# A LayerNorm chain over three chunks instead of two, with its input read a second time by halves

## The chip, the cores and the metric

The kernel runs on one core of a Trainium2 chip. The metric is device microseconds (us) of one execution. A core has five engines that run side by side: PE (TensorE, matmuls), DVE (VectorE), ACT (ScalarE), POOL (GpSimd) and SP (SyncE, which here only issues transfers). Each takes its own instructions in order. Transfers (DMA) run on 16 DMA engines; they are issued from SP's queue, a few from ACT's and POOL's. SBUF and PSUM are the on-chip memories, the second the one that matmuls write to; DRAM is outside.

## The reference, cut to what matters

Four images of 96 x 128 x 128 go through two layers. Layer 0 normalizes by groups, projects to 192 channels, convolves, and runs four directional scans (state space model). Their sum `ym` is normalized over its 192 channels pixel by pixel (LayerNorm), projected back to 96 channels and added to x. Layer 1 then works on that sum with convolutions and an attention whose products act as convolution weights. The change lies in the end of layer 0:

```python
yn = jnp.moveaxis(ym, 1, -1)
mu = yn.mean(-1, keepdims=True)
var = yn.var(-1, keepdims=True)
yn = (yn - mu) * jax.lax.rsqrt(var + 1e-05) * ln_w + ln_b
yn = jnp.moveaxis(yn, -1, 1)
return jnp.einsum('bdhw,cd->bchw', yn, out_w) + out_b[None, :, None, None]
...
x = x + _L0_conv_ref(_gn(x), ...)
x = x + _L1_conv_ref(_gn(x), ...)
```

## The kernel before, in words

The program is a sequence of generators whose steps are interleaved. `co_run(left, right, pace)` (L291) takes a step of `left`, whose `yield` gives a cost, and then steps of `right` until cost times pace is used up. Where LayerNorm stands in it:

- image 0: `ssm_output` and then `split_norm` are `left`, the scan of the second image pair (`ssm_scan`, steps of 2.6) is `right`, with a pace of 0.65 (L2501 and L2502). Up to the end of the scan the order of emission is kept on each engine (`in_order`, L328 and L2507).
- image 1: it is `right` beside `direct_maps` of image 0 (3 x 3 convolutions as matmuls, L2119), with a pace of 1.0 (L2512 to L2516).
- images 2 and 3: it is `right` beside the attention of the image before (matmuls of L1488 and L1503, evacuations from L1542 on), with a pace of 1.0 (L2544 to L2564), and followed by `split_norm` of the same image and `attn_output` of an earlier one.

From image 1 on, the tile framework orders the instructions of each engine itself, by emission and by its own estimate of when each is ready.

`ssm_output` (L924) takes an image in NS = 16 chunks of SN = 1024 pixels. The 192 channels lie as two halves (j = 0, 1) on 96 partitions. The mean is folded into the weights (`outws`), so that the projection can be made of the raw y and scaled afterwards. A chunk c goes through these steps:

- `load_y` (L936): y, 96 x 2 x 1024 float32, 768 KB, issued on SP; three buffers.
- `squares` (L941): the squares of each half, on ACT.
- `sums` (L946): matmuls of y and of the squares with a 32-column block of 1/192, in one bank of PSUM: mean and mean square of each pixel.
- `rows` (L960): ACT copies the bank to SBUF and issues two transfers that turn it into `mq`, 8 rows of 128 pixels for mean and mean square.
- `inverse` (L967) on DVE and `roots` (L973) on ACT: variance and its root; `back` (L977): the reciprocal on DVE, its transfer to DRAM (`rd`, issued on POOL), and the load of the input image `xr` on SP; `spread_out` (L993): `rd` read back to all 96 partitions as `r`, issued on POOL. L1072 adds the output's constant to `xr` on ACT.
- `projected` (L999): for each half h of 512 pixels two matmuls of y with `outws`; `scaled` (L1011): times r, on DVE; `added` (L1019): plus xr, on POOL; `counted` (L1027): statistics for the next layer, on DVE; then the store to `xnew` (L1078) on SP.

For images 1 to 3 (`turned`) the sum stands in `r`, for image 0 in `xr`. PSUM banks come from a pool of three for image 0 and of two for the others (L2509); the bank of the sums and those of the two projections take turns. In the loop (L1034) round c has the chunks new = c, mid = c - 1 and old = c - 2, and six pauses. Other tiles of `ssm_output` have two buffers, `st` one.

`split_norm` (L1081) then reads `xnew` twice; its second pass (L1247 among others) writes the planes that the attention reads.

Of the kernel before, what the change touches and what calls it, by code (L numbers as in the profile page):

```python
# [9 lines left out]
F32 = mybir.dt.float32  # L10
BF16 = mybir.dt.bfloat16
AF = mybir.ActivationFunctionType
# [5 lines left out]
C = 96  # L18
H = W = 128
L = H * W  # L20
CH = 512
NCH = L // CH
# [29 lines left out]
SN = 1024  # L52
NS = L // SN
# [16 lines left out]
def kernel(  # L70
# [26 lines left out]
    nc = tc.nc  # L97
# [180 lines left out]
    def bank(ps):  # L278

        return ps.tile([128, CH], F32, name="bank", tag="bank")  # L280

    def part(ps, *shape):
        n = 1
        for d in shape[1:]:
            n *= d
        t = bank(ps)[: shape[0], :n]
        return t if len(shape) == 2 else t.rearrange("p (a b) -> p a b", b=shape[2])
# [636 lines left out]
    def ssm_output(b, yms, xnew, stats, ps, side, turned):  # L924

        with tc.tile_pool(name="c2", bufs=2, side=side) as p2:  # L930
            xb = x[b].rearrange("c h w -> c (h w)")
            ym = yms.rearrange("(j p) l -> p j l", j=2)
            rd = dram.tile([L], F32, name="rd")
            ys, sums_of, near, made = {}, {}, {}, {}

            def load_y(c):  # L936
                if c < NS:
                    ys[c] = p2.tile([C, 2, SN], F32, name="y", bufs=3)
                    nc.sync.dma_start(ys[c], ym[:, :, bass.ts(c, SN)])

            def squares(c, j):  # L941
                sq = p2.tile([C, SN], F32, name="sq")
                nc.scalar.activation(sq, ys[c][:, j], AF.Square)
                sums_of[c, j] = sq

            def sums(c, j):  # L946
                sq = sums_of.pop((c, j))
                if j == 0:
                    sums_of[c] = bank(ps)
                pm = sums_of[c]  # L950
                for g in range(4):
                    rhs = sq if g % 2 else ys[c][:, j]
                    nc.tensor.matmul(
                        pm[32 * g : 32 * g + 32],
                        lhsT=mean192[:, 0:32],
                        rhs=rhs[:, bass.ts(g // 2, CH)],
                        start=(j == 0),
                        stop=(j == 1),
                    )
            def rows(c):  # L960
                st = p2.tile([128, CH], F32, name="st", bufs=1)
                nc.scalar.copy(st, sums_of.pop(c))
                mq = made[c] = p2.tile([RS, 2, W], F32, name="mq")
                for i in range(2):
                    nc.scalar.dma_start(mq[:, i], st[32 * i : 32 * i + 65 : 64])

            def inverse(c):  # L967
                m, q = made[c][:, 0], made[c][:, 1]
                nc.vector.tensor_mul(m, m, m)
                nc.vector.tensor_sub(q, q, m)  # L970
                nc.vector.tensor_scalar(q, q, 0.0, None, ALU.max)

            def roots(c):  # L973
                q = made[c][:, 1]
                nc.scalar.activation(q, q, AF.Sqrt, bias=eps[0:RS])

            def back(c):  # L977
                m, q = (made[c][:, i] for i in range(2))
                made.pop(c)
                if turned:  # L980
                    nc.vector.reciprocal(
                        m.rearrange("p (j t) -> p t j", j=TW), q.rearrange("p (t j) -> p t j", j=TW)
                    )
                    q = m
                else:
                    nc.vector.reciprocal(q, q)
                to = rd[bass.ts(c, SN)]
                nc.gpsimd.dma_start(to.rearrange("(p f) -> p f", f=W), q)
                xr = p2.tile([C, SN], F32, name="xr")
                nc.sync.dma_start(xr, xb[:, bass.ts(c, SN)])  # L990
                near[c] = xr, to

            def spread_out(c):  # L993
                xr, to = near[c]
                r = p2.tile([C, SN], F32, name="r")
                nc.gpsimd.dma_start(r, to.partition_broadcast(C))
                near[c] = xr, r

            def projected(c, h):  # L999
                po = part(ps, C, CH)  # L1000
                for j in range(2):
                    nc.tensor.matmul(  # L1002
                        po,
                        lhsT=outws[:, j],
                        rhs=ys[c][:, j, bass.ts(h, CH)],
                        start=(j == 0),
                        stop=(j == 1),
                    )
                return po

            def scaled(c, h, po):  # L1011
                r = near[c][1][:, bass.ts(h, CH)]
                if turned:
                    v = r.rearrange("p (h j t) -> p h j t", t=TN, j=TW)
                    nc.vector.tensor_mul(v, turned_view(po), v)
                else:
                    nc.vector.tensor_mul(r, po, r)  # L1017

            def added(c, h):  # L1019
                xr, r = (t[:, bass.ts(h, CH)] for t in near[c])  # L1020
                if turned:
                    v = r.rearrange("p (h j t) -> p h j t", t=TN, j=TW)
                    nc.gpsimd.tensor_add(v, v, turned_view(xr))
                else:
                    nc.gpsimd.tensor_add(xr, r, xr)

            def counted(c, h):  # L1027
                t = near[c][turned]
                nc.vector.bn_stats(stats[:, 2 * c + h], t[:, bass.ts(h, CH)])

            for c in range(3):
                load_y(c)
            yield 2.0
            for c in range(NS + 2):  # L1034
                new, old = c < NS, c - 2 if c >= 2 else None
                mid = c - 1 if 1 <= c <= NS else None
                if old is not None:
                    po = projected(old, 0)
                if mid is not None:
                    inverse(mid)  # L1040
                if new:
                    squares(c, 0)
                yield 1.2
                if mid is not None:
                    roots(mid)
                if old is not None:
                    scaled(old, 0, po)
                    po = projected(old, 1)
                    ys.pop(old)
                if new:  # L1050
                    squares(c, 1)
                yield 1.4
                if mid is not None:
                    back(mid)
                if old is not None:
                    added(old, 0)
                    scaled(old, 1, po)
                if new:
                    sums(c, 0)
                yield 1.4  # L1060
                if new:
                    sums(c, 1)
                if old is not None:
                    added(old, 1)
                    counted(old, 0)
                    load_y(c + 1)
                yield 1.4
                if new:
                    rows(c)
                if mid is not None:  # L1070
                    xr = near[mid][0]
                    nc.scalar.activation(xr, xr, AF.Identity, bias=outbs)  # L1072
                    spread_out(mid)
                if old is not None:
                    counted(old, 1)
                yield 1.4
                if old is not None:
                    nc.sync.dma_start(xnew[:, bass.ts(old, SN)], near.pop(old)[turned])  # L1078
                yield 1.4

    def split_norm(xnew, x1d, x2d, stats, keep, cnt, ps, side, planes, vector, done):  # L1081
# [174 lines left out]
    def turned_view(v):  # L1256

        return v.rearrange("p (h t j) -> p h j t", t=TN, j=TW)
# [1134 lines left out]
    class Image:  # L2393
# [26 lines left out]
        def norm(self, yms, ps, side):  # L2420
            yield from ssm_output(self.b, yms, self.xnew, self.stats, ps, side, self.b > 0)
# [47 lines left out]
    with tc.tile_pool(name="wp", bufs=1, side="left") as wp:  # L2469
# [7 lines left out]
        for images, pace in (([0], 0.25), ([1], 0.75), ([2, 3], 1.35)):  # L2477
            left = projections(images, weights, stats, wp, psl)
            if images[0] == 0:
                next(left)  # L2480
                next(others)
                made = pair_weights()
# [12 lines left out]
                wdt, wbc, outws, outbs = got  # L2495
# [148 lines left out]
```

## Time and profile before

| what | value |
|---|---|
| runs | 6549.08, 6573.5, 6575.6 us (median 6573.5) |
| profiled execution | 6572.02 us, span 6570.2 us |
| mean granted TensorE clock | 0.884 |
| busy PE, DVE, ACT, POOL | 5365.0, 4934.7, 3806.4, 3533.2 us (82, 75, 58, 54%) |
| DMA over the span | 1198.29 MB, mean 182 GB/s |
| squares L943 | 128, from 2110.5 to 5076.0 us |
| sums L953 | 2 x 512 matmul instructions |
| projection L1002 | 512 matmul instructions, 717 ns each in the mean |
| loads of y, L939 | 64 of 768 KB, 374 ns of SP each (median) |

A busy share is an average over stages with different limits, and a row that gives idle time names what the engine waited for before an instruction. A wait on one engine costs time only if the engine that bounds the stage is held by it. Windows are given in us from the span's start.

### The profile page before, as it was taken

To read this page: it belongs to the slowest core of one execution; us is meant where nothing else is said; L and a number is where in the kernel's file an instruction comes from. 1 tells how busy PE (TensorE), PEld (TensorE's weight loads), DVE (VectorE), ACT (ScalarE), POOL (GpSimd) and SP (SyncE) were. 2 spreads that over 40 slices of the span, in tenths; PEclk is the share of its full clock that TensorE was granted. 3 is DMA by queue.
4 is the path that set the end of the run, shared out by engine and by line. 5 is a ranking of instruction groups with operands and counts; after the bars stand their busy time and mean duration, and the time that the engine had idled before them with its cause. 6 is when DMAs were issued, how large, how long until landed. Compare 5 with 4: busy or idle time off the path is not lost. (4 is left out here: it accounts for less than half of the span.)

```text
span 6570.2 us, 76328 instructions
## 1 busy us (share of the span) xinstructions
PE 5365.0 (82%) x23264; PEld 2348.1 (36%) x23264; DVE 4934.7 (75%) x7469; ACT 3806.4 (58%) x4757; POOL 3533.2 (54%) x2744
## 2 busy tenths in 40 slices
PE   6889988987887835999987588876979777888888
PEld 2333323322222112444433244444424454344553
DVE  3247778988898768989745884687865788887867
ACT  1247768777787676677524464565544664444542
POOL 2236758978788546979522454466134574043430
PEclk9999989998998657999998799877988887998899
DMA  6767777776766757665676776655776555865658
GB/s 162 175 155 189 193 208 195 217 204 163 217 184 172 215 157 228 202 201 173 201 188 167 194 198 176 168 140 145 211 194 165 144 158 153 225 164 146 182 149 217
DMA packets 888486, 1198.29 MB, mean 182 GB/s; under 512 B 216142, under 2 KB 741014, under 8 KB 875596
## 3 DMA queue, kind: packets, MB, share of 16 engines
q1 hardware_dynamic: 864460, 1138.46, 63.7%
q0 software_dynamic: 16208, 38.42, 2.2%
q10 hardware_dynamic: 7408, 16.53, 0.8%
q8 instruction: 187, 3.06, 0.2%
q14 instruction: 223, 1.83, 0.1%
HBM read 777.62 MB, written 345.58 MB: 171 GB/s over the span
## 5 line engine op out<-in xcount | busy, mean ns | idle before, releaser
L622 PE MATMUL bank<-y,wp 128*128 128x512 f32 (+3 forms) x3584 | 1317.3, 626 | 86.3 <-DMA y<-y 33.8
L855 POOL TENSOR_TENSOR y<-y,dl 128x1024 f32<-128x1024 f32 x384 | 1058.0, 2755 | 271.8 <-DVE dl L847 252.6
L822 POOL TENSOR_TENSOR dl<-dl,u 128x1024 f32<-128x1024 f32 x384 | 1011.7, 2635 | 248.8 <-ACT dA L798 124.2
L843 DVE TENSOR_TENSOR_SCAN dA<-dA,pBC 128x512 f32<-128x512 f32 x768 | 981.4, 1278 | 30.7
L1488 PE MATMUL two<-ya,wd 128*64 128x192 f32 (+3 forms) x2376 | 600.6, 433 | 216.1 <-ACT odd L1559 106.8
L622 PEld LDWEIGHTS bank<-y,wp 128*128 128x128 f32 (+3 forms) x3584 | 459.0, 169 | 757.6 <-issue 656.0
L2119 PE MATMUL bank<-y,wn 128*128 128x384 f32 (+5 forms) x2408 | 678.0, 508 | 60.6 <-DMA y<-x1d 28.1
L847 DVE TENSOR_TENSOR dl<-dA,pBC 128x512 f32<-128x512 f32 x768 | 528.1, 688 | 257.6 <-PE pBC L736 185.0
L736 PE MATMUL pBC<-xr,wbc 60*128 60x512 bf16 (+1 forms) x1536 | 463.0, 405 | 316.4 <-DVE dA L843 245.3
L1922 ACT COPY yb<-ya 64x768 f32<-64x768 f32 (+1 forms) x660 | 537.9, 815 | 185.5 <-PE two L1488 122.1
L665 ACT ACTIVATE dl<-pd,dtb 128x512 f32<-128x512 f32 x768 | 486.2, 684 | 190.6 <-PE pd L736 175.2
L1488 PE MATMUL two<-yb,wd 128*64 128x192 f32 (+3 forms) x2376 | 573.3, 416 | 0.0
L826 DVE TENSOR_TENSOR pBC<-dl,pBC 128x512 f32<-128x512 f32 x768 | 527.6, 687 | 8.3 <-POOL dl L822 7.4
L2119 PEld LDWEIGHTS bank<-y,wn 128*128 128x128 f32 (+3 forms) x2408 | 310.7, 169 | 357.7 <-issue 194.1
L1488 PEld LDWEIGHTS two<-ya,wd 128*64 128x64 f32 (+1 forms) x2376 | 269.9, 174 | 433.3 <-ACT odd L1559 116.4
L798 ACT ACTIVATE dA<-dl,negA 128x1024 f32<-128x1024 f32 x384 | 420.3, 1141 | 2.3
L2226 POOL MEMSET o<- 1x1024 f32 x60 | 56.5, 949 | 602.8 <-PE bank L2281 296.0
L1992 POOL COPY own<-ring 32x512 f32<-32x512 f32 (+1 forms) x198 | 227.3, 1184 | 278.8 <-DVE ring L1581 237.1
L736 PEld LDWEIGHTS <-wbc 60*128 60x128 bf16 (+1 forms) x1536 | 103.2, 96 | 765.0 <-issue 752.0
L665 ACT ACT_TABLE_LOAD x248 | 318.2, 1283 | 97.4 <-PE pd L736 83.6
L1488 PEld LDWEIGHTS two<-yb,wd 128*64 128x64 f32 (+1 forms) x2376 | 298.2, 176 | 149.0 <-issue 41.1
L1002 PE MATMUL bank<-y,outws 96*96 96x512 f32 x512 | 298.3, 717 | 5.5 <-DVE r L1017 2.7
(323 smaller groups left out, 9888.6 us busy)
## 6 DMA issues: line engine op xcount, KB each, us to landing
u<-zb SPq DMA_DIRECT2D x192, 1024.0 KB
yms<-y SPq DMA_DIRECT2D x96, 512.0 KB
y<-yms SPq DMA_DIRECT2D x64, 768.0 KB
xn<-xnew SPq DMA_DIRECT2D x128, 384.0 KB
ya<-vp SPq DMA_DIRECT2D x120, 336.0 KB
y<-y SPq DMA_DIRECT2D x128, 258.2 KB
zb<-z SPq DMA_DIRECT2D x64, 512.0 KB
ya<-x1p SPq DMA_DIRECT2D x90, 336.0 KB
```

The costliest lines, as they stand in the source:

```text
L622: nc.tensor.matmul(blocks(pz[p:e]), lhsT=ws[k][:, d, c : c + e - p], rhs=window(ys[k], at, d, n), start=(i == 0), stop=(i == len(terms) - 1),)
L665: nc.scalar.activation(dst, src, AF.Softplus, bias=bias)
L736: nc.tensor.matmul(p, lhsT=w[rows], rhs=xr[rows, at : at + CH], start=True, stop=True)
L798: nc.scalar.activation(live[m]["dA"], live[m]["dl"], AF.Exp, scale=negA[:, g % 3, k : k + 1])
L822: nc.gpsimd.tensor_mul(t, t, u_view(n))
L826: nc.vector.tensor_mul(p, live[n]["dl"][:, bass.ts(half, CH)], p)
L843: nc.vector.tensor_tensor_scan(h, h, p, init, ALU.mult, ALU.add)
L847: nc.vector.tensor_mul(live[n]["dl"][:, sl], live[n]["dA"][:, sl], live[n]["C", half])
L855: nc.gpsimd.tensor_add(v, v, t.rearrange("p (a b) -> p a b", b=W))
L1488: nc.tensor.matmul(of(to[p:e], r), lhsT=w[:, i, c : c + e - p], rhs=tiles(t[k][PAIR[i]][:, SLOT[i]], o, r), start=(k == 0), stop=False,)
L1922: nc.scalar.copy(yb[k][64 * h - 64 : 64 * h, :, :n], ya[k][0:64, :, h * TN : h * TN + n])
L2119: nc.tensor.matmul(pc[p:e, :n].rearrange("p (h w) -> p h w", w=W), lhsT=w[:, c : c + e - p], rhs=v[:, :, 0:W], start=(i == 0), stop=(i == ...
```

## The change

The chain is drawn out: round c now has new = c, mid = c - 1, far = c - 2 and old = c - 3. `inverse` and `roots` stay with mid but come two and three steps later in the round, `back`, `spread_out` and the addition of the constant go to far, and projection and all after it to c - 3. The second half's `counted` is kept in `late` and called in the next round. The tile `y` has two buffers and is only read by `squares` and `sums`; the projection reads its own copy, `yh`, loaded by halves of 512 pixels (384 KB, two buffers) from the same place in DRAM. The next y is issued in the first step of a round and not in the fourth. The pauses are 4.0 at the start, then 7.8 a round (8.2 before) for 19 rounds (18 before), and 1.1 at the end. Nothing is changed in what is computed.

```diff
             def load_y(c):
                 if c < NS:
-                    ys[c] = p2.tile([C, 2, SN], F32, name="y", bufs=3)
+                    ys[c] = p2.tile([C, 2, SN], F32, name="y")
                     nc.sync.dma_start(ys[c], ym[:, :, bass.ts(c, SN)])
+
+            def load_half(i):
+                if i < NCH:
+                    again[i] = p2.tile([C, 2, CH], F32, name="yh")
+                    nc.sync.dma_start(again[i], ym[:, :, bass.ts(i, CH)])
...
             def projected(c, h):
                 po = part(ps, C, CH)
+                y = again.pop(2 * c + h)
                 for j in range(2):
                     nc.tensor.matmul(
                         po,
                         lhsT=outws[:, j],
-                        rhs=ys[c][:, j, bass.ts(h, CH)],
+                        rhs=y[:, j],
...
-            for c in range(3):
+            for c in range(2):
                 load_y(c)
-            yield 2.0
-            for c in range(NS + 2):
-                new, old = c < NS, c - 2 if c >= 2 else None
+                load_half(c)
+            yield 4.0
+            late = []
+            for c in range(NS + 4):
+                new = c < NS
                 mid = c - 1 if 1 <= c <= NS else None
+                far = c - 2 if 2 <= c <= NS + 1 else None
+                old = c - 3 if 3 <= c <= NS + 2 else None
+                if c > NS + 2:
+                    yield 1.1
+                    late.pop()()
+                    return
+                if far is not None:
+                    back(far)
                 if old is not None:
                     po = projected(old, 0)
-                if mid is not None:
-                    inverse(mid)
                 if new:
+                    if c:
+                        load_y(c + 1)
                     squares(c, 0)
-                yield 1.2
-                if mid is not None:
-                    roots(mid)
+                yield 1.1
                 if old is not None:
                     scaled(old, 0, po)
                     po = projected(old, 1)
-                    ys.pop(old)
+                if late:
+                    late.pop()()
                 if new:
                     squares(c, 1)
-                yield 1.4
+                yield 1.3
                 if mid is not None:
-                    back(mid)
+                    inverse(mid)
+                if far is not None:
+                    spread_out(far)
                 if old is not None:
                     added(old, 0)
                     scaled(old, 1, po)
...
                 if old is not None:
                     added(old, 1)
-                    counted(old, 0)
-                    load_y(c + 1)
-                yield 1.4
+                    load_half(2 * old + 2)
+                yield 1.3
+                if mid is not None:
+                    roots(mid)
+                if far is not None:
+                    xr = near[far][0]
+                    nc.scalar.activation(xr, xr, AF.Identity, bias=outbs)
+                if old is not None:
+                    load_half(2 * old + 3)
+                yield 1.3
                 if new:
                     rows(c)
-                if mid is not None:
-                    xr = near[mid][0]
-                    nc.scalar.activation(xr, xr, AF.Identity, bias=outbs)
-                    spread_out(mid)
                 if old is not None:
-                    counted(old, 1)
-                yield 1.4
-                if old is not None:
-                    nc.sync.dma_start(xnew[:, bass.ts(old, SN)], near.pop(old)[turned])
+                    counted(old, 0)
+                    nc.sync.dma_start(xnew[:, bass.ts(old, SN)], near[old][turned])
+                    late.append(lambda old=old: (counted(old, 1), near.pop(old)))
                 yield 1.4
```

More of the change, by code (lines that the diff above doesn't have):

```diff
@@ L933, in ssm_output @@
             rd = dram.tile([L], F32, name="rd")
-            ys, sums_of, near, made = {}, {}, {}, {}
+            ys, again, sums_of, near, made = {}, {}, {}, {}, {}
             def load_y(c):
                 if c < NS:
-                    ys[c] = p2.tile([C, 2, SN], F32, name="y", bufs=3)
+                    ys[c] = p2.tile([C, 2, SN], F32, name="y")
                     nc.sync.dma_start(ys[c], ym[:, :, bass.ts(c, SN)])
+            def load_half(i):
+                if i < NCH:
+                    again[i] = p2.tile([C, 2, CH], F32, name="yh")
+                    nc.sync.dma_start(again[i], ym[:, :, bass.ts(i, CH)])
             def squares(c, j):
```

## The prediction, made before the changed kernel ran

> **What bounds the kernel now.** The chain that ended last covers only the last 56 us of the span, so it says nothing of this change. I therefore found the four stretches in which LayerNorm runs (first to last square and store), and asked for the busy time of each engine in them. The columns are stretch, length, then busy time and instructions of each engine, the granted TensorE clock, the DMA share and GB/s.
>
> ```profile
> core 0: us, PE busy (x) PEld busy (x) DVE busy (x) ACT busy (x) POOL busy (x), PEclk, DMA share, GB/s
> 2110.00:2365.00 255.00, 192.52 (x492) 45.44 (x492) 173.97 (x232) 171.92 (x187) 134.98 (x99) 0.65 0.73 208
> 3100.00:3240.00 140.00, 131.42 (x569) 60.64 (x566) 119.31 (x147) 81.89 (x107) 106.39 (x51) 0.98 0.67 202
> 3240.00:3515.00 275.00, 242.03 (x911) 95.65 (x910) 129.75 (x336) 82.36 (x120) 75.76 (x109) 0.92 0.69 182
> 3935.00:4220.00 285.00, 248.92 (x1407) 120.72 (x1408) 156.91 (x297) 138.93 (x180) 128.94 (x155) 0.93 0.65 172
> 4830.00:5118.00 288.00, 249.24 (x1302) 112.07 (x1298) 157.95 (x283) 132.06 (x174) 135.02 (x165) 0.89 0.62 167
> ```
>
> Row 1 is image 0, beside the scan; row 2 is what runs just ahead of image 1, without LayerNorm; rows 3 to 5 are images 1 to 3. In images 1 to 3 PE is the bound, with 12 to 13.5% idle (33, 36 and 39 us), where row 2 has 6%. In image 0 no engine is full: it moves by waits. The waits of image 0, and of DVE in image 1:
>
> ```profile
> PE bank L953 <- ACT sq L943: 30.3, 10, 5.8
> DVE r L1017 <- DMA r<-rd: 21.9, 11, 4.0
> ACT xr L1072 <- DMA xr<-in_x: 20.3, 8, 5.0
> POOL rd L988 <- DVE mq L986: 90.5, 15, 8.9
> SPq L990 <- DMA xnew<-xr: 35.0, 13, 5.7
> SPq L724 <- DMA y<-yms: 17.0, 7, 2.9
> ...
> DVE mq L969 <- DMA mq<-st: 53.9, 10, 11.2
> DVE r L1015 <- DMA r<-rd: 20.2, 4, 7.3
> ```
>
> Columns: us in total, times, longest. An engine takes its instructions in order, so a step of LayerNorm that waits for its input holds everything behind it. PE pays for it at the sums, which miss their squares or a free bank. In image 1:
>
> ```profile
> L953 PE MATMUL bank<-y,mean 96*32 96x512 f32 x128 | 50.9, 689 | 20.1 <-DVE r L1015 9.4 <-DMA y<-yms 7.7 <-issue 2.9
> ```
>
> The DMA view of image 0's stretch (tenths in 40 slices, then the queue that SP fills):
>
> ```profile
> DMA  9497958359685955899368993888887397608476
> ...
> q1 hardware_dynamic: 21498, 46.48, 63.9%
> ...
> r<-rd POOLq DMA_DIRECT2D x16, 384.0 KB, 5.0
> ```
>
> DMA is full in about every second chunk, and half full in the other. The copies of the sums follow each other there by 12 and 17 us in turn (timeline of ACT); the long ones hold the scan's 1024 KB of u and its rows.
>
> **What the Trainium skill says.** "DMA: Bandwidth & Descriptors", section "Anatomy of one DMA", gives a transfer a fixed part of about 2 us, mostly completion, whatever its size. The trace agrees in kind: 4 KB of rd land in 3.5 us, 384 KB of r in 5.0. Two or three such landings stand in each chunk's chain, which more distance can cover. Its "Specifications" put the least row for line rate at 512 B; the new loads have rows of 2 KB, so I price them at the present mean rate. "SBUF — State Buffer", section "Who interferes with whom", says that a DVE instruction with two SBUF inputs blocks against a GpSimd one that reads SBUF. The trace fits: L969, 280 ns at the median, took up to 4.13 us. In image 0, L969 and L970 cost 29.2 us, some 20 over 32 x 280 ns. The change moves them beside other POOL work; I put nothing on it, and 20 us either way as its bound.
>
> **The change part by part.**
>
> *Distance.* inverse moves from the first to the third step of the round after its rows, roots to the fifth, back and spread_out to the round after that, and the projection a round later still. Waits for mq, roots, rd and r thus get two steps or more; the Identity on xr is four steps after its load instead of two. What goes on DVE, ACT and POOL is over 100 us an image (image 1: 53.9 + 20.2 on DVE, ACT 44.7 for L971, POOL 60.8 for L981), but off PE most of it is worth nothing. On PE the sums and projections waited 26.1 us in image 1 (20.1 + 3.2 + 2.8), 11.4 in image 2, 19.6 in image 3. Nor will all go: the two banks still turn in the same order, so that the sums wait for scaled(old, 0). I take half of these and some of the attention's own waits for DVE in images 2 and 3 (L1581 and L1667, 14.0 us in image 2): 14, 11 and 11 us. Bounds: 0 and 26, 22 and 24.
>
> *Counting.* counted(c, 1) moves to the next round, behind scaled. DVE waited for POOL before it 20.6, 63.8 and 39.1 us in images 1 to 3; this is part of the above.
>
> *y loaded a round ahead.* Before, y for c+1 was issued in the fourth step of round c, behind its buffer's release by the projection; now in the first, released by the sums. The waits of ACT for y (30.9 us, 14 times over all) go; image 0's 10.4 and the first load's 7.7 at image 1 (now behind a pause of 4.0, not 2.0) are in the sums here.
>
> *The second reading.* 128 loads of 384 KB, 50.3 MB on 1198.3. SP issues them at about 0.37 us (as y now), 12 us an image on a queue that has room. For the DMA engines: image 0's queue moved 46.48 MB in 0.639 x 255 = 163 us, 3.5 us a MB; 12.6 MB an image are 44 us (48 at image 2's rate: 0.566 x 285 / 42.31 = 3.8). The shares become about 0.90, 0.86, 0.82 and 0.79. In images 1 to 3 I hide it in the open slices. If that cover goes, up to 20 us an image: a load of 768 KB more, 2.7 us, in half of the 16 rounds.
>
> *Image 0* has less cover. Its transfers of all queues take 0.73 x 255 = 186 us; with 44 more it is 230 of 255, so the chunk can't go below 14.4 us against 15.9 now, even with DMA always full. Here SP also stands: xr's load now heads the round, and must wait for xnew's store just before it (2.7 us a time, 35.0 / 13) and for counted(c, 1) of the chunk whose buffer it takes, which is one step away. Behind it stand y, yh, and the scan's u, rows and stores; the scan holds these three to six steps ahead. yh has most of a round from its release, with u in the queue ahead in the long rounds: PE may wait 0 to 3 us there, 8 times. Against it stand the 30.3 us of PE waiting for squares, 21.9 and 20.3 for r and xr. I take 5 us slower; bounds 20 faster, 30 slower.
>
> *Pace.* 2.0 + 18 x 8.2 = 149.6 becomes 4.0 + 19 x 7.8 + 1.1 = 153.3, so a little more of the partner's work is put beside each image. In the built order, image 1's last projection stands behind 1095 of the 1204 matmuls of L2119, before 1074; image 2's behind 566 of L1488, before 504. Work is moved, not added. But what follows image 1 is DVE's (3600 to 3700: over 85% busy, PE once idle for 41.2 us behind the split's L1247), and begins when LayerNorm ends: 21 matmuls ahead of it take back some 9 of the 14 us. For images 2 and 3 the split after it has DVE at 85% (196 of 230 us), so less attention there does no harm.
>
> *The sum:* +5 (image 0), -14 + 9 = -5, -11, -11: -22 us. The profiled execution took 6572.0 us (span 6570.2), 1.5 under the median of 6573.5. So 6550 on the profile, 6551 us as a median, -0.3%: inside the 0.5% (33 us) that I take as what a measurement of this kernel can tell.
>
> **The rivals.**
>
> A, *clearly faster*: the stalls of PE go nearly whole. 26 + 22 + 24 from images 1 to 3 less 9, and 15 from image 0 (12-us chunks become the rule): -78, 6495; with two thirds of it, 6522. For it: row 2 shows that PE can run at 6% idle. Against: DMA, and the unchanged bank order. Chance 0.33.
>
> B, *slower*: the second reading finds no room. Place: the long rounds of image 0, where DMA is full, and image 1, whose L2119 takes nine small loads a chunk from the same queue. Price: 2.7 us in each of the 16 rounds of image 0 (43 us) and in half of those of the others (3 x 20), less about half of the gain on PE above (18): +85, 6658 at worst; with half of the price, 6607. It decides once a round's transfers outlast its engines, which is at a DMA share of about 0.95; image 0 comes to 0.90 by the sum. For it: PE has waited 22.5 us for y<-x2d and 13.6 for y<-x1d just after image 1. Chance 0.30.
>
> C, *it does not lengthen the distance where it counts*: outside image 0 the order on each engine is made by a planner from estimates, and P and S (projection, sums) now stand as one block of PE. If the bank waits stay, nothing is gained: 6573 to 6580. This lies in "no change".
>
> **Numbers.** Forecast with C 0.37; A 0.33; B 0.30. The likeliest case alone: 6540 to 6595. The range reaches into A and B: 6505 to 6620.
>
> **What would show it.** Right: waits for mq<-st and r<-rd near zero on DVE; POOL at rd near zero; L953 on PE waiting under 10 us an image; DMA share 0.8 to 0.9 in the four stretches; image 0 as long as before. Wrong: PE waiting for yh, SP standing at xr's load, image 0 over 280 us (B), or any stretch of images 1 to 3 with PE over 94% busy (A).

## The result, and the profile after

The changed kernel takes 6665.5 us in the median of four runs (6656.75 to 6671.41), against 6574.55 for the kernel before beside it: a ratio of 1.0146, 95% interval 1.0118 to 1.0174. It is about 90 us slower. Forecast were 6551, with a range of 6505 to 6620, so it lies above the range. In a second comparison (experiment `after5` below) the ratio is 1.0160 (1.0143 to 1.0178); the experiments are measured against that one.

The same stretches as before, first square to last store of images 0 to 3, in the busy-time view of the changed kernel (stretch, length, busy time and instructions by engine, granted clock, DMA share, GB/s):

```profile
core 0: us, PE busy (x) PEld busy (x) DVE busy (x) ACT busy (x) POOL busy (x), PEclk, DMA share, GB/s
2104.00:2393.00 289.00, 180.73 (x493) 45.99 (x494) 166.72 (x234) 171.80 (x187) 137.60 (x100) 0.63 0.82 227
3255.00:3567.00 312.00, 253.56 (x965) 105.31 (x965) 135.23 (x326) 83.66 (x122) 79.12 (x117) 0.86 0.77 202
3980.00:4300.00 320.00, 278.94 (x1649) 143.71 (x1649) 173.55 (x335) 157.37 (x207) 149.24 (x188) 0.93 0.77 200
4905.00:5220.00 315.00, 272.66 (x1498) 133.90 (x1498) 176.85 (x333) 150.64 (x197) 151.97 (x185) 0.92 0.77 201
```

Every stretch is longer. But a stretch also holds the partner's work (1649 matmuls beside image 2, 1407 before), so its length is no price. I price by distances between fixed points of the program in the two profiled executions: first load of y to last store for image 0; from there the end of the scan (L843), and the first softmax instruction of each image's attention (L1706, now L1725; softmax 1 is the first image's).

| stage | before | after |
|---|---|---|
| image 0, first load of y to last store | 260.4 | 294.4 |
| end of the scan to softmax 1 (holds image 1) | 414.2 | 462.2 |
| softmax 1 to 2 (holds LayerNorm of image 2) | 916.5 | 905.5 |
| softmax 2 to 3 (rest of the split, output, image 3) | 962.0 | 986.1 |
| softmax 3 to 4 | 821.1 | 817.9 |

Stages without the change differ by up to some 14 us from one profiled execution to the next (softmax 1 to 2 takes 916.5 here, and 908.9 and 902.2 in two experiments below that leave images 2 and 3 as they were), so single entries are read no finer than that. The loss stands in image 0 (34), in image 1 (48) and behind softmax 2 (24).

In image 0 the waits view now has this (engine, line, releaser: us in total, times, longest):

```profile
PE bank L1008 <- DMA yh<-yms: 85.8, 14, 12.0
DVE r L1023 <- PE bank L1008: 84.2, 17, 12.2
...
PE bank L958 <- ACT sq L948: 6.3, 4, 3.7
```

The wait that the change was to shorten, PE for the squares, fell from 30.3 to 6.3 us. In its place PE stands 85.8 us at the projection for the second reading, and DVE as long for PE. SP's own waits say why the reading is late:

```profile
SPq L995 <- DMA xnew<-xr: 87.5, 12, 11.7
...
SPq L995 <- DVE xstats L1035: 17.2, 7, 3.3
```

L995 is the load of xr, now ahead of y and yh in a round. One such round in the timeline of SP's queue, and of PE (start, us, line, output and input; in brackets the idle time ahead):

```profile
2265.17 0.52 SPq L1096 DMA_DIRECT2D xnew<-xr  x1
2279.39 0.33 SPq L995 DMA_DIRECT2D xr<-in_x  x1
2279.83 0.37 SPq L939 DMA_DIRECT2D y<-yms  x1
2280.30 0.88 SPq L944 DMA_DIRECT2D yh<-yms  x2
```

```profile
2274.31 6.09 PE L1008 MATMUL bank<-yh,outws 96*96 96x512 f32 x8 [11.97 <-DMA yh<-yms]
...
2288.44 2.87 PE L1008 MATMUL bank<-yh,outws 96*96 96x512 f32 x3 [5.00 <-DMA yh<-yms]
```

The store to `xnew` is issued at 2265.17. The load of xr, whose buffer that store reads, follows it directly and cannot start for 14 us; y and yh, which need nothing of it, stand behind it in the same queue. y is late by most of this. yh is late by less: its two buffers come free only with the projections that start at 2274.31 (their matmuls end at 2278.0 and 2280.4 in the trace), so that SP issues the first half 2.3 us late here. Over the whole stretch the 30 halves behind the first two go out 82 us after their buffers came free, in sum; most go in pairs, so that by an estimate the stretch can lose about half of that.

SP stood no longer than before, only elsewhere. The waits at the store itself, before and after the change:

```profile
SPq L1078 <- POOL xr L1025: 94.1, 13, 9.9
```

```profile
SPq L1096 <- POOL xr L1031: 25.7, 8, 7.4
```

With the load of xr these are 94.1 + 35.0 = 129 us before and 25.7 + 87.5 + 17.2 = 130 now. What is new is that yh, which the projection needs within a round, stands behind the wait.

In image 1 PE waits elsewhere than before (waits view, 3255 to 3567):

```profile
PE bank L2138 <- DMA y<-x1d: 26.0, 3, 10.9
PE bank L1008 <- DMA yh<-yms: 25.5, 9, 8.5
...
PE bank L958 <- DVE r L1021: 3.2, 3, 1.6
```

The wait of the sums for `scaled` fell from 9.4 to 3.2 us; the wait for yh is new. That for y<-x1d, the partner's own input, was 4.1 us in this stretch before, but much of the rise is moved: from the end of the scan to softmax 1 PE waits 40.2 us for y<-x1d and y<-x2d before and 47.5 now. Behind image 1, from the end of L2138 to softmax 1, there was a stretch of 10 us; now it has 34, with DVE busy throughout and PE nearly idle:

```profile
3687.00:3720.50 33.50, 2.93 (x13) 1.95 (x12) 33.45 (x75) 11.11 (x16) 21.88 (x29) 0.58 0.53 142
```

### The profile page after: what moved, and what is told of

It is laid out like the page before. It is cut to its first block, busy times and chain, and to the rows that moved or that the text cites. A ratio compares the mean times of both kernels' runs of the same rounds, so it can differ in the third digit from the quotient of the medians.

```text
span 6655.0 us, 76541 instructions
## 1 busy us (share of the span) xinstructions
PE 5341.8 (80%) x23264; PEld 2363.9 (36%) x23264; DVE 4923.0 (74%) x7469; ACT 3804.9 (57%) x4756; POOL 3521.7 (53%) x2744
## 5 line engine op out<-in xcount | busy, mean ns | idle before, releaser
L843 DVE TENSOR_TENSOR_SCAN dA<-dA,pBC 128x512 f32<-128x512 f32 x768 | 981.5, 1278 | 30.6
L2138 PE MATMUL bank<-y,wn 128*128 128x384 f32 (+5 forms) x2408 | 682.6, 508 | 79.3 <-DMA y<-x1d 51.3
L2138 PEld LDWEIGHTS bank<-y,wn 128*128 128x128 f32 (+3 forms) x2408 | 312.6, 169 | 380.3 <-issue 187.7
L1008 PE MATMUL bank<-yh,outws 96*96 96x512 f32 x512 | 298.4, 730 | 111.3 <-DMA yh<-yms 111.3
```

What stands on the lines that cost most here:

```text
L843: nc.vector.tensor_tensor_scan(h, h, p, init, ALU.mult, ALU.add)
L2138: nc.tensor.matmul(pc[p:e, :n].rearrange("p (h w) -> p h w", w=W), lhsT=w[:, c : c + e - p], rhs=v[:, :, 0:W], start=(i == 0), stop=(i == ...
```

## The experiments

Theory 1: in image 0 it is SP's order, xr's load ahead of y and yh behind its own store. Theory 2: the transfers of the second reading have no room. Theory 3: in images 1 to 3 it is the place of LayerNorm among the partner's instructions. A ratio is to the kernel before on the same chip, whose median lay between 6548 and 6572 us, so experiments are compared by ratios. One thousandth is 6.6 us.

### Which image costs what

Both loops stand in one kernel, the one before with its three buffers of y, and a constant chooses by image: `(0,)` in `three0`, `(1,)` in `three1`, `(2, 3)` in `three23`.

```diff
+            two = b not in (0,)
...
+            if two:
+                for c in range(3):
+                    load_y(c)
...
+                return
             for c in range(2):
                 load_y(c)
```

> Three chunks and the second reading in image 0 alone; images 1 to 3 as before the change. Read off the two traces, image 0 costs 34 us (last store 27.9 later, first load 6.1 earlier). If the shares are independent, this kernel takes 34 over before, about 6608. If the losses seen after image 0 are only what image 0's delay does to the later stages, the whole 91 us show here: about 6660.

> The changed loop in image 1 alone. If image 1's 48 us (softmax of image 1 minus that of image 0, between the traces) are its own, from its own queue and its own place among the partner's matmuls, about 6622. If they are a consequence of image 0, near 6570 as forecast for image 1 (-5).

> The changed loop in images 2 and 3 alone. From the traces: image 2 gives 11 us, image 3 gives about 11, and 24 us are lost between the two in the split and the last steps of image 0 on that side: about 6587. If the 24 us are a consequence of the earlier images, 6552.

Measured: 1.0022 (1.0011 to 1.0033) for image 0 alone, 1.0063 (1.0052 to 1.0075) for image 1, 1.0037 (1.0024 to 1.0050) for images 2 and 3: 14, 41 and 24 us. Each part costs by itself; the losses of images 1 to 3 are no consequence of image 0. The sum is 80, the whole 105.

Image 0 alone fits neither number: its stretch is 293.3 us as in the changed kernel, and its scan ends some 35 us later than in the two others, but the program loses only 14. Why the rest is given back later there I did not settle.

The loss behind softmax 2 is real, and the 11 us that image 2 seemed to gain are not. Where images 2 and 3 are as before (`three0`, `three1`), softmax 1 to 2 takes 908.9 and 902.2 us and softmax 2 to 3 takes 964.5 and 970.6; in `three23` these are 910.4 and 988.6.

### SP's order in image 0

The tile xr and its load move from `back`, in the first step of a round, to a function `load_x` that image 0 calls in the fifth; the Identity on xr goes to the first step of the next round. Image 0 only.

```diff
-                xr = p2.tile([C, SN], F32, name="xr")
-                nc.sync.dma_start(xr, xb[:, bass.ts(c, SN)])
-                near[c] = xr, to
+                near[c] = None, to
+                if not behind:
+                    load_x(c)
...
                     load_half(2 * old + 3)
+                if far is not None and behind:
+                    load_x(far)
```

> The changed kernel, but in image 0 SP issues xr's load as the last of a round's loads, behind y and both yh, instead of first; its Identity goes to the next round. Theory 1 (SP stands at xr's load for the store of xnew just before it, and y and yh stand behind it): SPq at xr's load falls from 87.5 us for xnew to under 20, PE's 85.8 us for yh to under 30, image 0 is 20 to 30 us shorter, the time about 6638. Theory 2 (the transfers of the second reading have no room, DMA at 0.82): the wait moves to another load and image 0 stays within 5 us of 289, the time 6660.

Measured: 1.0114 (1.0101 to 1.0127), 30 us less than the changed kernel. Image 0 takes 265.4 us instead of 294; SP no longer waits for xnew at xr's load. The busy-time row and DMA lines of its stretch:

```profile
2096.00:2362.00 266.00, 174.35 (x500) 45.16 (x497) 174.90 (x242) 171.79 (x187) 142.62 (x102) 0.67 0.91 250
```

```profile
DMA  8949599999989999899998999689996997787647
...
DMA packets 30650, 66.37 MB, mean 250 GB/s; under 512 B 2968, under 2 KB 14142, under 8 KB 30638
```

Theory 1 holds for half of image 0's loss. DMA now is busy for 9 tenths or more in 24 of the 40 slices (15 in the changed kernel), and PE still waits 50.1 us for yh in 9 waits, more than the 30 that theory 1 allowed.

### The second reading left out

In `once` for all images, in `once0` for image 0 alone, by a condition on the image (the edit is that of `once`):

```diff
             def load_half(i):
-                if i < NCH:
+                if 2 <= i < NCH:
+                    again[i] = again[i - 2]
+                elif i < 2:
                     again[i] = p2.tile([C, 2, CH], F32, name="yh")
```

> The changed kernel without the second reading: only the first two halves of y are loaded, and every projection of the image reads one of these two (so the output is another one); all else stays, with its order. Theory 2 (no room for the transfers, in image 0 and image 1): PE's waits for yh go by construction, and its waits for y<-x1d in image 1 (26.0) too, the time falls by 45 or more, to 6605 or less. Theory 1 (in image 0 it is the order on SP's queue): y itself still stands behind xr's load, image 0 gains 10 to 20. Theory 3 (in images 1 to 3 it is where LayerNorm's end stands among the partner's instructions): images 1 to 3 gain under 15; the time 6625 to 6640.

> The changed kernel with the second reading left out in image 0 alone (its projections read the first two halves; the output of that image is another one). Without the second reading in all images, the scan beside image 0 ended 55 us earlier than in the changed kernel (3202.7 against 3257.4). If that is image 0's own and stays, 6600. If image 0's time is partly given back later, as in the kernel with three chunks in image 0 alone (34 us in the stage, 16 at the end), 6625 to 6635.

Measured: `once` 0.9992 (0.9983 to 1.0001), `once0` 1.0064 (1.0052 to 1.0076). Without the second reading the change costs nothing: 110 us go, where theory 2 set 45 or more and the two others 10 to 20 in image 0 and under 15 in images 1 to 3. 63 us belong to image 0 (1.0160 - 1.0064) and 47 to images 1 to 3 (1.0064 - 0.9992). Image 0's saving stays, against the second guess. The stretch of image 0 in `once`:

```profile
2101.00:2339.00 238.00, 170.27 (x498) 42.10 (x497) 176.39 (x241) 171.38 (x187) 142.66 (x102) 0.73 0.80 230
```

238 us, 22 less than before the change (18 to 21 less than in `three1`, `three23` and `b1025`, whose image 0 is as before): this is what the drawn-out chain is worth there, with the earlier y and the new pauses in it. SP still stands at xr's load for xnew:

```profile
SPq L997 <- DMA xnew<-xr: 73.9, 12, 10.8
```

So most of this wait, 6.2 us a time against 7.3 in the changed kernel, is there without the bytes of the second reading. It still holds y up (PE waits 31.6 us for y at the sums), but no yh any more. What it costs here was not tried.

Outside image 0 the built order changes with the second reading, although the expectation took it as kept. Where images 1 to 3 lose their 47 us shows in the stages: `once` against `once0` 441.9 and 461.5 us for the end of the scan to softmax 1, 1874.7 and 1894.1 for softmax 1 to 3, 814.2 and 823.5 behind it. In images 2 and 3 no PE wait for yh is recorded. There it seems to be the order: with the second reading the built order puts image 2's last projection behind 566 matmuls of L1488, without it behind 504, where it stood before the change, at the same pauses (image 1's stands behind 1093 and 1072 of L2119 in the traces). DVE pays, at `scaled`, between softmax 1 and 3. First `once`, then `once0`:

```profile
DVE r L1023 <- DMA r<-rd: 32.3, 9, 9.9
...
DVE r L1023 <- PE bank L1010: 12.0, 5, 6.2
```

```profile
DVE r L1023 <- PE bank L1010: 70.7, 21, 14.9
...
DVE r L1023 <- DMA r<-rd: 8.7, 2, 6.6
```

Both waits together are 44 us without and 79 with the second reading. That this later projection, and not the transfers, costs the 28 us of images 2 and 3 is argued from these waits; I did not force the old order with the transfers kept.

### Bytes or number of loads

On top of `xrlate0`:

```diff
-                    again[i] = p2.tile([C, 2, CH], F32, name="yh")
-                    nc.sync.dma_start(again[i], ym[:, :, bass.ts(i, CH)])
+                    n = 2 if turned else 1
+                    again[i] = p2.tile([C, n, CH], F32, name="yh")
+                    nc.sync.dma_start(again[i], ym[:, 0:n, bass.ts(i, CH)])
...
-                        rhs=y[:, j],
+                        rhs=y[:, j if turned else 0],
```

> The kernel with xr's load behind y and yh in image 0 (1.0114 of before), where in image 0 each second load brings only one of the two rows j (192 KB instead of 384; both products of the projection then use this row, so that image's output is another one). Number, order and places of the loads stay. If the 27 us that image 0 still stands above the kernel without second reading (265 against 238) are for bytes, half of them go: image 0 at about 252, the ratio 1.0093. If they are for the loads' number or order, image 0 stays at 265, the ratio at 1.0114.

Measured: 1.0089 (1.0075 to 1.0103), 16 us less than `xrlate0`, and image 0 at 245.2 us:

```profile
2094.00:2340.00 246.00, 176.50 (x501) 44.95 (x498) 172.94 (x243) 171.59 (x187) 142.62 (x102) 0.69 0.85 244
```

Without half of the second reading's bytes (60.07 MB instead of 66.37 in the stretch), 20 of the 27 us are gone, with as many loads in the same places; about half were expected. So the other half of image 0's loss is for the bytes and not for the number of loads, as theory 2 had it.

Why the bytes cost is less sure, since a rival to "no room" was not tried: the two buffers of yh hold one chunk, so that a half can't be issued before the projection one chunk earlier has freed its buffer. In the trace of `xrlate0` 19 of the 30 halves behind the first two go out within 0.25 us of that, and are used 6.5 to 16.8 us after their issue (all 30 together 35 us after their buffers came free, against 82 in the changed kernel). The second reading is thus the one step whose distance was not drawn out, and PE waits for its landing in 9 of the 16 chunks. Fewer bytes shorten this landing whether DMA is full or not; a third buffer for yh would tell the two apart.

### The place in images 1 to 3

The pauses of the loop are multiplied by a constant `quick`; a pause is the cost by which the partner's steps are dealt out. It is 0.90 in `pace90`, 0.976 in `pace976`, and 0.976 in image 1 alone in `pace1`.

```diff
+            quick = 0.90 if turned else 1.0
...
-            yield 4.0
+            yield 4.0 * quick
```

> The changed kernel with all pauses of LayerNorm in images 1 to 3 times 0.90, so that its last projections stand at 1070 matmuls of L2119 and 500 and 1351 of L1488 in the built order (before 1074, 504, 1344; changed kernel 1095, 566, 1391). Theory 3: the DVE tail behind L2119's end (33.9 us, before 10.3) and the 24 us between the softmax of image 1 and norm of image 3 go: 40 less, about 6615. Theory 2: the chain is squeezed into fewer partner matmuls, PE's waits for yh and y<-x1d grow by what is saved: within 10 of the changed kernel.

> The same with 0.976, which undoes the 2.5% that the pauses' sum grew by (153.3 to 149.6): last projections at 1071, 548 and 1385. Theory 3: image 1's tail goes (its place is undone), the loss between images 2 and 3 only by a third: 25 to 35 less, about 6625. Theory 2: within 10 of the changed kernel.

> The changed kernel with the pauses times 0.976 in image 1 alone. If the 36 us of the shorter pauses came from image 1's place among the partner's DVE instructions, 6620 to 6628. If images 2 and 3 gave a good part of it, 6635 to 6645.

Measured: 0.976 gives 1.0100 (1.0087 to 1.0114), 39 us less than the changed kernel; in image 1 alone 1.0108 (1.0095 to 1.0121), 34 less; 0.90 gives 1.0170 (1.0152 to 1.0187), no gain, the number that theory 2 had. So nearly all of the 39 us are image 1's. The tail, as I call the stretch from the end of L2138 to softmax 1, is 15 and 16 us in the two 0.976 kernels, 34 in the changed one. With 0.90 the tail goes too (8 us), but L2138 ends 28 us later than with 0.976, and softmax 1 to 3 is longer by 28. Theory 2's waits don't explain it: PE waits longer for the partner's own y (30.4 and 21.9 us for x1d and x2d, against 22.2 and 13.4), but less for yh (16.6 against 36.9). Theory 3 is right for the tail and wrong as a rule that an earlier LayerNorm is better; why 0.90 loses stays open.

Is it the pauses by themselves? The kernel before, with the pauses of image 1 times 1.025 and nothing else:

> The kernel before, with its pauses in image 1 times 1.025 (149.6 to 153.3) and nothing else. In the built order of DVE softmax 1 then stands at instruction 3737, as with three chunks in image 1 (3737), against 3706. If the DVE tail comes from the pauses' sum alone, the softmax follows L2119's end by 34 us instead of 10 and the time is 20 to 30 us above before (1.003 to 1.0046). If it needs three chunks or the second reading, 1.000.

Measured: 1.0028 (1.0017 to 1.0038), 18 us, with a tail of 34.0 us (3609.5 to 3643.5). Here is this tail, and then that of `three23`, where image 1 is as before:

```profile
3609.00:3643.50 34.50, 3.72 (x18) 2.33 (x16) 34.44 (x78) 11.55 (x16) 20.28 (x35) 0.55 0.54 144
```

```profile
3610.00:3620.40 10.40, 2.63 (x17) 1.75 (x15) 10.40 (x19) 5.08 (x8) 10.27 (x12) 0.82 0.81 228
```

There are 78 DVE instructions instead of 19 between the last map matmul and the softmax. In the built order softmax 1 is DVE's instruction 3737 instead of 3706. The 31 that went ahead of it are, but for one, those of `pixel_planes` (L1445 to L1454 of the kernel before), called from `lift` in the partner's `direct_maps`; in `three23` they run behind softmax 1. So it is not LayerNorm's own work, or the split's, that went ahead. A sum of pauses that is 2.5% longer does this alone, with two chunks and one reading.

### The changed kernel again

> The changed kernel once more, beside the experiments: 6650 to 6665. The three parts alone cost 12, 36 and 22 us over before; if they add up it is at 6627, and what lies above that comes from one part acting on the next.

Measured: 6655.31 us, 1.0160 (1.0143 to 1.0178). That is 105 us, 25 above the sum of the three parts, with an uncertainty of some 18; how the parts act on each other I did not follow further.

### The remedies together

> Both remedies in the changed kernel, nothing left out: in image 0 xr's load behind y and yh, and in images 1 to 3 the pauses times 0.976. Alone they gave 30 and 36 us. If the two losses are independent, 6655 - 66 = 6589. If one hides the other, 6605 to 6620. In neither case below the kernel before (6553): the transfers of the second reading are still there.

> The kernel without the second reading in any image (only two halves of y are read again; 6548), with the pauses of images 1 to 3 times 0.976. In the built order of DVE softmax 1 stands at instruction 3706 before the change, 3736 with it, 3736 without the second reading, 3707 with the shorter pauses. If the DVE tail behind L2119 (34 us with or without the second reading, 10 before) is due to this place alone, 20 to 30 less: 6518 to 6528. If it needs the transfers too, 6545.

`xr976` is `xrlate0` with the pauses of images 1 to 3 times 0.976: 1.0066 (1.0050 to 1.0081), 62 us less than the changed kernel where the two alone gave 30 and 39. Within the uncertainty they add up. It is the best of the kernels that keep the three chunks and the whole computation, and still 43 us slower than before.

`once976` is `once` with the same pauses: 0.9963 (0.9949 to 0.9978), 24 us faster than before and 19 less than `once`. This is what the drawn-out chain would bring if y had not to be read again. It would need y to be kept in more buffers; whether there is room for them was not looked into, and this was not tried on the chip.

The ratios make one account, each line the step from one kernel to the next (10 to 14 us of uncertainty a line):

| part | from, to | us |
|---|---|---|
| chain drawn out (three chunks, earlier y), without second reading | before, `once976` | -24 |
| the pauses' place in images 1 to 3, softmax 1 on DVE above all | `once976`, `once` | +19 |
| second reading in images 1 to 3, with the order that it brings | `once`, `once0` | +47 |
| second reading in image 0 | `once0`, changed | +63 |
| ... of this SP's order | `xrlate0`, changed | 30 |
| ... of this the reading itself, with two buffers | `once0`, `xrlate0` | 33 |
| sum | before, changed | +105 |

## Why the prediction was wrong

**Image 0: forecast +5, measured +34 in its stretch.** The failed step is the sentence on SP at xr's load. The wait was seen, with what stands behind it, but priced at "2.7 us a time (35.0 / 13)", the wait before the change. It came to 7.3 (87.5 / 12). The second reading's bytes are not the main reason, since without them it is still 6.2 (73.9 / 12 in `once`). The new place is, as far as the edit tells (it was not tried by itself): before, three pauses (1.4, 1.2, 1.4) lay between the store and the load that waits for it, now one of 1.4. From that followed in part the second mis-sized term, "PE may wait 0 to 3 us there, 8 times", at most 24 us: it is 85.8 us in 14 waits, 6.1 each. "yh has most of a round from its release" is true, but its landing needs that round: even with xr's load moved PE waits 50.1 us. The bound of 30 slower was too small. The third is the bytes: they were worked out (44 us more on a stretch of 255), then set against a full-time floor of 230 us, as if 90% of DMA's time could be used without a wait; at a share of 0.91 PE still waited 50 us. What I set against it was right in kind: the waits for squares went, and the chain gives 22 us here without the second reading. With xr's load moved the stretch is 265.4 us, 5 above before, as forecast; but as the sum of some -22 and +27 that the prediction had not priced so, which is luck.

**Image 1: forecast -5, measured +48 in its stage.** "In images 1 to 3 I hide it in the open slices" failed: PE waits 25.5 us for yh, and the stage is 461.5 us with the second reading (`once0`) and 441.9 without (`once`). And the step "21 matmuls ahead of it take back some 9" looked at PE, where the place was decided on DVE: 30 instructions of the partner's planes ahead of the softmax, 24 us of tail. The trace of before showed DVE full there; I should have looked the softmax up in DVE's order. With both remedies image 1's stage is 431.8 us (`xr976`), without the second reading and with the shorter pauses 427.1 (`once976`), against 414.2 before; what is left of it stays open.

**Images 2 and 3: forecast -22, measured a loss.** The PE waits at the sums fell as forecast (those for `scaled` from 10.7 to 5.0 us and from 9.8 to 1.4), but no time came of it: softmax 1 to 3 is 1899.0 us in `three23`, where `three0` and `three1` have 1873. The failed step is to count these waits as time. I knew that the last projection stood behind 566 instead of 504 matmuls and wrote that "less attention there does no harm".

**Distance.** Waits of DVE for mq in image 1 fell from 53.9 to 38.3 us, not to near zero, and those for r from 20.2 to 2.7, replaced by 39.9 for the projection's bank. POOL at rd still waits 97.4 us there. All told the drawn-out chain is worth 24 us without the second reading, about what image 0's stretch alone gains (22). "I take half of these" failed for images 1 to 3: in `once`, where no yh delays PE, the sums wait 18.0, 14.2 and 20.8 us for `scaled` between the same points, against 9.4, 10.7 and 9.8 before. The banks still turn in the same order, as the prediction itself set against it.

**The rivals.** B was right in place: the second reading costs, in image 0 first. Whether it is for want of room, as B had it, or for yh's two buffers is open. It priced 43 us there and 60 in the others, where 63 and 47 were measured; the 19 us of place were not in it, nor was SP's order as the cause of half of image 0's. Its threshold was wrong: it was to decide above a DMA share of 0.95, and the loss came at 0.82, in half because of SP's order, and was still 33 us with a share of 0.91. C was right that the bank waits of images 1 to 3 stay without the second reading; the place of the projections it read as no gain, not as a loss.

The Trainium skill, "DMA: Bandwidth & Descriptors", section "Specifications", gives some 358 GB/s as one core's limit for DRAM. Here (`xrlate0`, image 0) DMA was 0.91 busy at 250 GB/s, with nearly half of the packets under 2 KB. So the page's figure was no measure of the room in this mixture; the share said more, though PE waited for yh at 0.82 already.

## What to carry to other kernels

Price a moved load by what stands behind it in its queue, and take the wait at its new place, not the one it had: a load that waits for the store just ahead of it costs through what follows it, and here yh did. A second reading needs distance of its own: with two buffers of half a chunk its landing stood in the loop, and PE waited 85.8 us for it at a DMA share of 0.82 and 50.1 at 0.91. So set the transfers' time against the stretch with a margin. And where a partner's steps are dealt out by costs, look at every engine's order behind the change, the one that is full there first: a sum of pauses 2.5% longer cost 18 us with no other edit.

## What had not been expected of the hardware

With the same instructions in image 0, DMA moved 227 GB/s at a share of 0.82 when SP's queue was held up, and 250 at 0.91 when it was not; without the second reading it was 230 at 0.80 in a stretch 56 us shorter. The place of one load in a queue that only issues transfers was thus worth 30 us.
